# Decoder attention with rotary embedding: halves of each head from a second projection, or swapped by DMA from the third block on

## The chip, the cores and the metric

The kernel runs on one core of a Trainium2 chip. A core has five engines with queues of their own, each in order: PE (TensorE, matmuls into PSUM), DVE (VectorE), ACT (ScalarE), POOL (GpSimd) and SP (SyncE, which here only issues DMAs). They meet through semaphores. DMAs issued by SP, ACT or POOL move data beside them. The metric is the device time of one execution in microseconds (us), lower is better; the time of a kernel is the median of several runs. All times below are from the start of the profiled span.

## The reference, cut to what matters

A network of four layers, each a graph attention over 2708 nodes with a dense adjacency, followed by a feed-forward part that differs from layer to layer. The change touches only the feed-forward part of the third layer, a decoder block: causal attention over the 2708 nodes as one sequence (T = 2708, C = 256, 4 query heads and 2 key heads of 64), with a rotary embedding of q and k, and then a mixture of eight experts, two for each node.

```python
def _rotate_half(x):
    h = x.shape[-1] // 2
    return jnp.concatenate([-x[..., h:], x[..., :h]], axis=-1)
...
h = _rmsnorm(x, ln1_w)
q = (h @ wq.T).reshape(Bx, Tx, NH, HD).transpose(0, 2, 1, 3)
k = (h @ wk.T).reshape(Bx, Tx, NKV, HD).transpose(0, 2, 1, 3)
v = (h @ wv.T).reshape(Bx, Tx, NKV, HD).transpose(0, 2, 1, 3)
q = q * cos + _rotate_half(q) * sin
k = k * cos + _rotate_half(k) * sin
...
scores = jnp.einsum('bhtd,bhsd->bhts', q, k) / jnp.sqrt(jnp.float32(HD))
scores = jnp.where(causal[None, None], scores, jnp.float32(-1e+30))
att = jax.nn.softmax(scores, axis=-1)
y = jnp.einsum('bhts,bhsd->bhtd', att, v).transpose(0, 2, 1, 3).reshape(Bx, Tx, Cx)
x = x + y @ wo.T
```

## The kernel before

All numbers are float32. The whole network is one program; the function `attention` (line 1981) does the decoder's attention and calls the experts at its end.

**Tiling.** The 2708 nodes are cut into six column blocks, n = 0 to 5: five of 512 nodes and a last one of 148 (`cols`). Queries of a block are handled against all key tiles of 128 nodes up to the diagonal. A step (n, p, j) is one block n, one pair p of query heads and one key tile j. A pair holds one query head for each of the two key heads, each on 64 of the 128 partitions. In blocks 0 to 4 the two pairs are separate; in block 5 both go in one step (m = 2).

**A step.** `scores` multiplies the key tile with the queries on PE (line 2108, `sc`), takes the exp on ACT (line 2117, `e`) and masks diagonal tiles on VectorE (line 2123). `values` multiplies V with `e` on PE (line 2133, `po`) and adds `e` to a running sum on VectorE (line 2139, `sum`). `e` has four buffers, which are free again when that sum has read them. After a pair's last key tile, `close` sums over partitions on PE (`pd`, line 2147) and divides on VectorE (lines 2152 and 2153, `yt`).

**The projection of a block.** `project(n)` (line 2035) is a generator, run in small pieces between the steps of the block before. It norms the block's rows, transposes them (`tp`, line 2052, copied to `ft` by ACT, line 2056), projects V (`pv`, copied by ACT at line 2063), and then for k and the two pairs of q does this: for m = 0 and m = 1 it multiplies `ft` with columns of the weight into PSUM (line 2079, `pj`), the columns for m = 1 being those of m = 0 with the halves of each head exchanged; VectorE multiplies the two products with the cosine and with the signed sine (line 2082, `kt` or `qt`, and `tmp`); GpSimd adds the two (line 2083). The tables come by a DMA on ACT's queue (`rope`, line 2039).

**Closing work.** `send(n)` (line 2155) takes a closed block through the output projection (`wy`, line 143 in the trace as the matmuls are made by a helper; line 2170 on VectorE adds the residual, `xa`; line 2171 on GpSimd adds into X), the second norm (`h`, line 2183, and the chain of small operations `rr` in `inverse_root`), the router (`pr`, `dlogits`, line 2208) and `route.chunk`, which finds each node's slots (`rank`, `dto`) and scatters its rows to `hs` in DRAM by indirect DMAs on GpSimd's queue (line 1759). `route.keep` stores X to DRAM on SP's queue (line 1792, `dys<-X`). After block 2 (`CUT`), `route.cut` fixes the first eight expert tiles, and `route.load` reads them from `hs` on SP's queue (line 1907, `X<-hs`, eight loads of 130 KB).

**What sets the order.** On PE the order is the program's, written out by hand: `scores` of two steps, a piece of `send`, `values` of the two steps before, `close`, and then as many pieces of `project` as the count at line 2278 allows (its factor of 18 spreads the pieces over the steps of a block). On the other engines and on SP a scheduler orders the instructions ahead of time. `pj`, `pv`, `tp`, `pr`, `wy` and `pd` share one PSUM pool of two buffers (`aux`), used in turn. `tmp` has two buffers.

**After the attention.** When block 5 has been projected, `last_project` closes the pools of the projection, and `weights.more` loads the experts' w1 (line 1621) into the room that they leave; w3 follows at the attention's end. The experts (`h`, line 2349) start then.

Of the kernel before, what the change touches and what calls it, by code (L numbers as in the profile page):

```python
# [8 lines left out]
F32 = mybir.dt.float32  # L9
# [3 lines left out]
ALU = mybir.AluOpType  # L13
# [3 lines left out]
P = 128  # L17
# [31 lines left out]
def tiles_of(start, length):  # L49
    return range(start // P, (start + length + P - 1) // P)  # L50
# [1930 lines left out]
def attention(net, route, ln2, router, weights, mixture):  # L1981
# [7 lines left out]
    nc, tc, a, X = net.nc, net.tc, net.a, net.X  # L1989
    G, DH, CUT = 2, 64, 2  # L1990
    cols = chunks(512)
    halves = (slice(0, DH), slice(DH, P))
    with ExitStack() as ctx:
# [5 lines left out]
        aux = core.enter_context(tc.tile_pool(name="a_x", bufs=2, space=PSUM))  # L1999
# [5 lines left out]
        for t0, t1 in ((0, 4), (4, 12), (12, NT)):  # L2005
            g = slice(t0, t1)
# [28 lines left out]
        def project(n):  # L2035
            i0, iw = cols[n]
            its = tiles_of(i0, iw)
            rope = pp.tile([P, 2, 512], F32, name="rope")
            nc.scalar.dma_start(rope[:, :, :iw], a["rope"][:, :, i0 : i0 + iw].rearrange("n p i -> p n i"))
            ft = pp.tile([P, 2, 512], F32, name="ft")  # L2040
            fs = {}
            for t in its:
                fs[t] = pp.tile([P, D], F32, name="f", bufs=4)
                net.normed(fs[t], t, (ln[0], both))
            yield
            for k in range(0, len(its), 2):
                pair = its[k : k + 2]
                ps = aux.tile([P, 2, 2 * P], F32, name="tp", tag="aux")
                for m, t in enumerate(pair):
                    r, f = rows(t), fs[t]  # L2050
                    for c in range(2):
                        nc.tensor.transpose(
                            ps[:, c, m * P : m * P + r], f[:r, c * P : (c + 1) * P], net.ident[:r, :r]
                        )
                nw = (len(pair) - 1) * P + rows(pair[-1])
                nc.scalar.copy(ft[:, :, k * P : k * P + nw], ps[:, :, :nw])
                yield
            ps = aux.tile([P, 4, G, DH], F32, name="pv", tag="aux")
            for k, t in enumerate(its):
                r = rows(t)  # L2060
                net.matmul_k(ps[:r, k].rearrange("p g d -> p (g d)"), ft[:, :, k * P : k * P + r], wv)
            for k0, k1, r in whole_and_rest(its):
                nc.scalar.copy(V[:r, its[k0] : its[k1 - 1] + 1], ps[:r, k0:k1])

            if n + 1 < len(cols):
                queries[n] = [qp.tile([P, 1, 512], F32, name=f"qt{p}") for p in range(2)]
                pairs = [q[:, 0, :] for q in queries[n]]
            else:
                queries[n] = [qp.tile([P, 2, iw], F32, name="qt0")]
                pairs = [queries[n][0][:, p, :] for p in range(2)]  # L2070
            for dst, w in [(kt[:, i0 : i0 + iw], wk)] + [
                (pairs[p], wq[:, :, p * 2 * P : (p + 1) * 2 * P]) for p in range(2)
            ]:
                yield
                tmp = pp.tile([P, 512], F32, name="tmp")
                for m, part in enumerate((dst, tmp[:, :iw])):
                    ps = aux.tile([P, 512], F32, name="pj", tag="aux")
                    for c in range(2):
                        nc.tensor.matmul(  # L2079
                            ps[:, :iw], w[:, c, m * P : (m + 1) * P], ft[:, c, :iw], start=c == 0, stop=c == 1  # L2080
                        )
                    nc.vector.tensor_tensor(part, ps[:, :iw], rope[:, m, :iw], ALU.mult)
                nc.gpsimd.tensor_tensor(dst, dst, tmp[:, :iw], ALU.add)

        def by_pairs(t, m, iw):

# [160 lines left out]
        with tc.manual_schedule(engines={mybir.EngineType.PE}):  # L2247
# [10 lines left out]
            for group in groups + [[]]:  # L2258
                while group and group[-1][0] not in ready:
                    next(heads)  # L2260
                if group and group[0][0] > at[0]:
                    at[:] = group[0][0], 0, 0
                for step in group:
                    exp = scores(*step)
                next(tails, None)
                for step in before:
                    values(*step)
                if at[0] + 1 == len(cols):
                    next(tails, None)
                quiet -= 1  # L2270
                for n, p in ending:
                    close(n, p)
                    quiet = 2
                    if p + 1 == len(queries[n]):
                        closed.append(n)
                ending = [(n, p) for n, p, j in before if j == tiles_of(*cols[n])[-1]]
                at[1] += 1
                while group and at[2] * len(queries[at[0]]) * (tiles_of(*cols[at[0]])[-1] + 1) < at[1] * 18:
                    if quiet > 0 and at[0]:
                        break  # L2280
                    at[2] += 1
                    next(heads, None)
                before = group
# [434 lines left out]
```

## Time and profile before

| | |
|---|---|
| median of three runs | 2539.14 us (2534.76 to 2540.16) |
| the profiled execution | 2543.42 us |
| its span on the core | 2541.7 us |
| PE busy | 2403.5 us, 95% |
| VectorE busy | 1495.4 us, 59% |
| ACT busy | 1058.9 us, 42% |
| GpSimd busy | 438.9 us, 17% |
| decoder attention, first projection to experts | about 1496 to 1861 us |
| projections `pj` (line 2079) | 144 matmul records, 1496.0 to 1793.1 us |
| their multiplies on VectorE (line 2082) | 36, 0.69 us each for 128x512 |
| their adds on GpSimd (line 2083) | 18, 1.27 us each for 128x512 |
| `sc` and `po` of a group of two full steps on PE | 1.99 and 1.94 us |

Each float32 matmul shows as two records on PE. A line of the timeline has the start, the length from the first start to the last end, the engine, the line, the operation with its tiles and shapes and the number of records; idle time of the engine ahead of it stands in brackets with what ended it. As matmuls overlap, what a group costs is best taken from its start to the next group's start. A row of a stretch has its length and, for each engine, busy time and count. The waits list who waited for whom: total, times, longest.

### The profile page before, as it was taken

To read this page: it belongs to the slowest core of one execution; us is meant where nothing else is said; L and a number is where in the kernel's file an instruction comes from. 1 tells how busy PE (TensorE), PEld (TensorE's weight loads), DVE (VectorE), ACT (ScalarE), POOL (GpSimd) and SP (SyncE) were. 2 spreads that over 40 slices of the span, in tenths; PEclk is the share of its full clock that TensorE was granted. 3 is DMA by queue.
4 is the path that set the end of the run, shared out by engine and by line. 5 is a ranking of instruction groups with operands and counts; after the bars stand their busy time and mean duration, and the time that the engine had idled before them with its cause. 6 is when DMAs were issued, how large, how long until landed. Compare 5 with 4: busy or idle time off the path is not lost.

```text
span 2541.7 us, 32517 instructions
## 1 busy us (share of the span) xinstructions
PE 2403.5 (95%) x11437; PEld 1565.4 (62%) x11437; DVE 1495.4 (59%) x3446; ACT 1058.9 (42%) x1762; POOL 438.9 (17%) x581
## 2 busy tenths in 40 slices
PE   6899998989999999989899999999989999979999
PEld 5567665677233334568678864434467777757887
DVE  7753346837799996335544457788862222243666
ACT  3444443323788882332444333334422222234444
POOL 1000003201221222244230001222232122210011
PEclk9999999969899999989999999999999999989999
DMA  8899612000374764676520010001342222150001
GB/s 281 294 296 342 208 47 74 1 6 1 65 106 84 96 100 146 168 180 218 199 79 1 1 32 25 28 26 43 114 126 42 34 34 34 26 169 7 1 1 44
DMA packets 130276, 240.10 MB, mean 94 GB/s; under 512 B 10941, under 2 KB 76052, under 8 KB 127274
## 3 DMA queue, kind: packets, MB, share of 16 engines
q1 hardware_dynamic: 97440, 162.11, 20.0%
q0 software_dynamic: 29680, 71.77, 14.2%
q10 hardware_dynamic: 2990, 4.06, 0.6%
q8 instruction: 97, 1.59, 0.3%
q14 instruction: 69, 0.57, 0.1%
HBM read 146.52 MB, written 91.37 MB: 94 GB/s over the span
## 4 chain that ended last, share of the span: by engine, by line
PE 81%; DVE 10%; DMA 4%; ACT 2%; issue 1%; POOL 1%; SPq 0%; DVEq 0%; ACTq 0%; POOLq 0%
PE acc L1535 15%; PE acc L941 8%; PE h L2349 8%; PE acc L311 7%; PE po L2381 4%; PE score L298 4%; PE den L951 3%; PE y L1279 3%; PE sc L2108 3%; PE pv L143 3%; PE po L2133 3%; PE h L1138 3%; PE pj L2079 2%; DVE sum L2139 2%; DMA dys<-y,to 2%; PE po L143 2%
## 5 line engine op out<-in xcount | busy, mean ns | idle before, releaser
L1535 PE MATMUL acc<-V,e 128*128 128x257 f32 x1848 | 404.3, 381 | 5.8 <-DVE e L737 5.8
L1535 PEld LDWEIGHTS acc<-V,e 128*128 128x128 f32 x1848 | 351.3, 190 | 58.5 <-issue 6.6
L737 DVE SCALAR_TENSOR_TENSOR e<-e,low,mask 128x1172 f32<-128x1172 f32 (+1 forms) x176 | 273.7, 1622 | 21.4 <-ACT e L736 21.3
L736 ACT ACTIVATE e<-big_p,minus,ratio 128x1172 f32<-128x1172 f32 (+1 forms) x176 | 250.5, 1504 | 44.9 <-PE den L951 44.2
L737 DVE SCALAR_TENSOR_TENSOR e<-e,mask 128x768 f32<-128x768 f32 (+1 forms) x176 | 153.6, 875 | 171.2 <-ACT e L736 170.1
L736 ACT ACTIVATE e<-big_p,minus_one,ratio 128x768 f32<-128x768 f32 (+1 forms) x176 | 166.2, 947 | 210.5 <-PE acc L1535 189.9
L2349 PE MATMUL h<-w,ft 128*128 (+1 forms) x720 | 222.1, 450 | 0.0
L311 PE MATMUL acc<-F,e 128*128 128x257 f32 (+1 forms) x924 | 212.5, 383 | 4.2 <-DVE e L307 3.8
L941 PE MATMUL acc<-e,V 128*64 128x512 f32 (+1 forms) x1056 | 209.6, 549 | 1.3 <-DVE e L737 1.3
L311 PEld LDWEIGHTS acc<-F,e 128*128 128x128 f32 (+1 forms) x924 | 171.6, 189 | 57.0 <-DVE e L307 29.7
L2366 DVE TENSOR_TENSOR hh<-hh,h 128x682 f32<-128x682 f32 x47 | 40.7, 867 | 240.4 <-PE h L2349 240.4
L941 PEld LDWEIGHTS acc<-e,V 128*64 128x64 f32 x1056 | 73.7, 138 | 150.5 <-issue 146.0
L307 DVE TENSOR_TENSOR e<-e,mask 128x512 f32<-128x512 f32 (+2 forms) x132 | 80.4, 621 | 139.4 <-ACT e L300 137.7
L2349 PEld LDWEIGHTS h<-w,ft 128*128 128x128 f32 x720 | 129.1, 189 | 52.2
L2117 ACT ACTIVATE e<-sc 128x1024 f32<-128x1024 f32 (+4 forms) x131 | 107.4, 862 | 116.7 <-PE sc L2108 91.7
L2139 DVE TENSOR_TENSOR sum<-sum,e 128x1024 f32<-128x1024 f32 (+4 forms) x131 | 138.2, 1055 | 19.6 <-PE po L2133 11.4
L300 ACT ACTIVATE e<-score 128x512 f32<-128x512 f32 (+2 forms) x132 | 69.4, 544 | 171.0 <-PE score L298 145.5
L2381 PE MATMUL po<-w,ht 114*128 (+1 forms) x564 | 129.7, 379 | 0.9 <-DVE ht L2374 0.9
L2108 PE MATMUL sc<-qt,kt 64*128 64x512 f32 (+5 forms) x568 | 121.6, 546 | 1.4 <-ACT sum L2117 0.9
L2381 PEld LDWEIGHTS po<-w,ht 114*128 114x128 f32 x564 | 106.5, 189 | 22.6 <-DVE ht L2374 8.3
L298 PE MATMUL score<-QK 128*128 128x512 f32 (+2 forms) x264 | 112.1, 553 | 3.4 <-ACT e L300 3.0
L2133 PE MATMUL po<-e,V 128*64 128x512 f32 (+5 forms) x524 | 107.5, 527 | 1.7 <-DVE e L2123 1.7
(686 smaller groups left out, 3664.3 us busy)
## 6 DMA issues: line engine op xcount, KB each, us to landing
row<-in_adj SPq DMA_DIRECT2D x21, 1354.0 KB
raw<-in_adjT SPq DMA_DIRECT2D x35, 768.0 KB
sums<-e POOLq DMA_DIRECT2D x76, 330.0 KB
hs<-zero SPq DMA_DIRECT2D x8, 2860.0 KB
mask<-kept SPq DMA_DIRECT2D x42, 338.5 KB
hidden<-hr SPq DMA_DIRECT2D x32, 256.0 KB
wd<-in_f_wd SPq DMA_DIRECT2D x8, 1024.0 KB
kept<-mask SPq DMA_DIRECT2D x21, 338.5 KB
```

Of the source, the lines that this page charges most:

```text
L143: self.nc.tensor.matmul(out, lhsT[:, c, :], rhs[:, c, :], start=first and c == 0, stop=last and c == n - 1)
L298: nc.tensor.matmul(ps[:r, :iw], QK[:, 0, span(j)], QK[:, 1, i0 : i0 + iw], start=True, stop=True)
L311: ended = nc.tensor.matmul(acc[k], e[:r, k * P : (k + 1) * P], F[:r, j, :], start=j == 0, stop=j == NT - 1)
L736: nc.scalar.activation(v, big_p[:, i], AF.Relu, bias=minus, scale=ratio)
L737: return nc.vector.scalar_tensor_tensor(v, v, plus, net.mask[:, j, i], ALU.add, ALU.mult)
L941: nc.tensor.matmul(acc[n][half, :iw], V[:, j, h, :], e[n][:, k, :iw], start=j == 0, stop=j == NT - 1)
L1535: nc.tensor.matmul(acc[k][:ri], e[:, k * P : k * P + ri], V[:, j, :], start=j == 0, stop=j == NT - 1)
L2108: nc.tensor.matmul(by_pairs(ps[:r, g], m, iw)[:, :, o:], kt[b, span(j)], qt[b, :, o:iw], start=True, stop=True)
L2133: nc.tensor.matmul(by_pairs(outs[n, p][b], m, iw)[:, :, o:], V[:r, j, g, :], by_pairs(e[:r, g], m, iw)[:, :, o:], start=j == 0, stop=j == ...
L2139: nc.vector.tensor_tensor(total, total, by_heads(e[:r], m, iw)[:, :, :, o:], ALU.add)
L2349: last = nc.tensor.matmul(halves[s, n][:, q, :HALF], fts[s][:, c, :], weights.w13[n][:, es[s], c, q * HALF : (q + 1) * HALF], start=c == 0 ...
L2381: last = nc.tensor.matmul(ps, ht[:KP, k, :], w2[:KP, es[s], k, :], start=k == 0, stop=k == KC - 1)
```

## The change

From block 2 on, the second product (m = 1) is not computed. ACT copies the first product from PSUM to a new tile `plain` (two buffers), four DMAs on SP's queue copy 32 partitions each from `plain` to `tmp` with neighbouring groups of 32 exchanged, and VectorE multiplies `tmp` with the sine table in place. This multiply and GpSimd's add are put off: they are called in the next piece of the projection (`waiting`), those of the last pair in one more piece at the end. The count of pieces has the factor 20 instead of 18. Blocks 0 and 1 keep both products. The weights keep the exchanged columns.

```diff
--- before.py
+++ after.py
@@ -2068,19 +2068,40 @@
             else:
                 queries[n] = [qp.tile([P, 2, iw], F32, name="qt0")]
                 pairs = [queries[n][0][:, p, :] for p in range(2)]
+            waiting = []
             for dst, w in [(kt[:, i0 : i0 + iw], wk)] + [
                 (pairs[p], wq[:, :, p * 2 * P : (p + 1) * 2 * P]) for p in range(2)
             ]:
                 yield
                 tmp = pp.tile([P, 512], F32, name="tmp")
-                for m, part in enumerate((dst, tmp[:, :iw])):
-                    ps = aux.tile([P, 512], F32, name="pj", tag="aux")
+
+                def product(m):
+                    ps = aux.tile([P, 512], F32, name="pj", tag="aux")[:, :iw]
                     for c in range(2):
-                        nc.tensor.matmul(
-                            ps[:, :iw], w[:, c, m * P : (m + 1) * P], ft[:, c, :iw], start=c == 0, stop=c == 1
-                        )
-                    nc.vector.tensor_tensor(part, ps[:, :iw], rope[:, m, :iw], ALU.mult)
-                nc.gpsimd.tensor_tensor(dst, dst, tmp[:, :iw], ALU.add)
+                        nc.tensor.matmul(ps, w[:, c, m * P : (m + 1) * P], ft[:, c, :iw], start=c == 0, stop=c == 1)
+                    return ps
+
+                def turned(dst=dst, tmp=tmp[:, :iw], src=None):
+                    nc.vector.tensor_tensor(tmp, tmp if src is None else src, rope[:, 1, :iw], ALU.mult)
+                    nc.gpsimd.tensor_tensor(dst, dst, tmp, ALU.add)
+
+                ps = product(0)
+                if n > 1:
+                    plain = pp.tile([P, 512], F32, name="plain")
+                    nc.scalar.copy(plain[:, :iw], ps)
+                    for g in range(0, P, 32):
+                        nc.sync.dma_start(tmp[g : g + 32, :iw], plain[g ^ 32 : (g ^ 32) + 32, :iw])
+                nc.vector.tensor_tensor(dst, ps, rope[:, 0, :iw], ALU.mult)
+                if n > 1:
+                    for late in waiting:
+                        late()
+                    waiting[:] = [turned]
+                else:
+                    turned(src=product(1))
+            if n > 1:
+                yield
+            for late in waiting:
+                late()
 
         def by_pairs(t, m, iw):
 
@@ -2275,7 +2296,7 @@
                         closed.append(n)
                 ending = [(n, p) for n, p, j in before if j == tiles_of(*cols[n])[-1]]
                 at[1] += 1
-                while group and at[2] * len(queries[at[0]]) * (tiles_of(*cols[at[0]])[-1] + 1) < at[1] * 18:
+                while group and at[2] * len(queries[at[0]]) * (tiles_of(*cols[at[0]])[-1] + 1) < at[1] * 20:
                     if quiet > 0 and at[0]:
                         break
                     at[2] += 1
```

The compiled order of the changed program, set beside the one before: on PE nothing but the `pj` groups, `pv` of blocks 3 and 4 and the last block's second q projection has another place, `pj` being halved from block 2 on (the two q projections of block 2 now stand together). On SP the twelve swaps of block 2 stand ahead of the first `dys<-X`, twelve ahead of the second, eight ahead of the third, then four, the eight `X<-hs`, the four swaps of k of block 5, the fourth `dys<-X`, the last eight swaps and the loads of w1.

## The prediction

> **What bounds the kernel now.** I read the shares and the chain of waits first: PE is busy 95% of the span and 81% of the chain that ended last, so time is lost or won where PE's queue gets shorter or waits. Then I cut the decoder attention into stretches (columns: length, then busy time and count of PE, PEld, DVE, ACT and POOL, clock, DMA share, GB/s):
>
> ```profile
> 1545.00:1595.00 50.00, 49.22 (x228) 22.69 (x226) 38.60 (x77) 19.44 (x30) 6.92 (x7) 1.00 0.07 22
> 1595.00:1660.00 65.00, 63.42 (x294) 27.75 (x292) 51.97 (x117) 25.41 (x39) 16.98 (x15) 1.00 0.08 28
> 1660.00:1745.00 85.00, 82.03 (x372) 33.47 (x370) 67.48 (x162) 33.93 (x49) 17.35 (x15) 1.00 0.06 19
> 1745.00:1815.00 70.00, 69.33 (x338) 29.32 (x334) 59.58 (x136) 31.73 (x45) 18.65 (x18) 1.00 0.35 123
> ```
>
> In these 270 us, where all that the change touches runs, PE is busy for 264.0, DVE for 217.6 (81%), ACT for 110.5 (41%). PE bounds, at clock 1.00; DVE is close behind, ACT is not. Blocks are counted as in the code, n = 0 to 5; the change acts on n = 2 to 5.
>
> **What is removed.** PE's timeline gives a projection as eight matmul records, four of which are the second product:
>
> ```profile
> 1604.80 3.70 PE L2079 MATMUL pj<-ft,wk 128*128 128x512 f32 x8
> 1608.43 1.99 PE L2108 MATMUL sc<-qt,kt 64*128 64x512 f32 x8
> ...
> 1757.09 1.27 PE L2079 MATMUL pj<-ft,wk 128*128 128x148 f32 x8
> 1758.30 1.99 PE L2108 MATMUL sc<-qt,kt 64*128 64x512 f32 x8
> ```
>
> From start to next start a full block's costs 3.63 us, so half is 1.81; the last block's costs 1.21, half is 0.60. Blocks 2, 3 and 4 drop nine halves (16.3 us), block 5 three (1.8 us): **18.1 us** of PE, all in its own queue. Two waits for a PSUM buffer of the same pool also shrink: 1.57 us ahead of the q projection at 1631.12 (the order of instructions now puts VectorE's add `xa` earlier there; I take 0.9 as gone) and 0.58 at 1792.64, whose projection moves forward. Together -19.6 us.
>
> **What is added beside other work.** Twelve ACT copies out of PSUM: nine at 0.585 us (the row `V<-pv` 128x512), three shorter, under 6 us together. ACT idles for 101 us of the 270 behind PE's scores, which hides them: nothing. If that cover went, each would hold the next exp by at most 0.6 us, 6 us in all. VectorE keeps its count: the second multiply reads SBUF instead of PSUM, 0.691 us for the PSUM form against 0.684 for a row of the same size that reads SBUF alone (`sum<-sum,e` 128x512): nothing. GpSimd's twelve adds stay, later. The extra step per block and the factor 20 for 18 move projections by a step or two in PE's order and add no instruction.
>
> **The swaps.** 48 DMAs on SP's queue, four to a tile. One issue costs 0.43 us (median of `X<-hs`). No row shows an SBUF-to-SBUF transfer of 64 KB; the nearest is a 128 KB load on the same queue, from issue to the first instruction that uses it:
>
> ```profile
> 2258.32 4.70 SPq L1974 DMA_DIRECT2D X<-dys  x9
> ...
> 2260.44 0.43 DVE L164 BATCH_NORM_STATS2 bnst<-X 128x6 f32<-128x256 f32 x1 [5.93 <-DMA X<-dys]
> ```
>
> That is 2.1 us. The other bound is the 512 KB `dys<-X` on this queue, at the 300 to 400 GB/s that the w1 load reaches about 1.5 us of moving more, 3.6 us; I take 2.1, whose size is nearest. So a tile is swapped 0.6 + 3 x 0.43 + 2.1 = 4.0 us after its product. The late multiply waits for it on VectorE, whose queue is in order: everything behind stands too, above all the running sums (which free the exp buffers) and `xa` (which frees PSUM for PE). I placed each late multiply in the order that the changed program has on VectorE, and compared. For k of block 2 both come at about 1555; q pair 0 of block 2 waits some 1.9 us where VectorE now idles 2.22 us for `wy`; q pair 1 has 10 us to spare; for k of blocks 3 and 4 the swap is late by 0.4 to 1.2 us; for q pair 0 of blocks 3 and 4 it arrives within 0.3 us of the end of the sum ahead of it; q pair 1 of both has 1 us or more, also in block 4, where its swaps stand on SP behind the store `dys<-X` (1710.16); both q pairs of block 5, pair 0 again behind a `dys<-X`, are late by about 0.5 to 1. I put 2 us on all eleven (0 if they arrive 0.5 us sooner, 9 if 1 us later). Behind the swaps on SP come only those stores and the loads of w1, which go when the last add is done (1795 today) and are needed at 1861: 45 us of cover beyond the 20 or so that they take. The multiply of q pair 0 now also lies between the last sums and the reciprocals of a closing pair, a place where PE waits in block 4 (1.90 us for `yt`): +0.7 us.
>
> **The twelfth, k of block 5,** is another matter. In SP's new order its four swaps stand behind the eight loads `X<-hs`, which wait for scattered rows:
>
> ```profile
> SPq L1907 <- DMA hs<-h,dto: 55.0, 1, 55.0
> ```
>
> ```profile
> 1751.87 1.92 POOL L1759 DMA_INDIRECT hs<-h,dto  x1 [35.54 <-DVE h L1757]
> ...
> 1763.07 1.02 POOL L1759 DMA_INDIRECT hs<-h,dto  x1 [0.30 <-issue]
> ```
>
> ```profile
> 1765.57 3.67 SPq L1907 DMA_DIRECT2D X<-hs  x8
> ```
>
> The scatters start when VectorE has the slots, take GpSimd 12 us, and only then do the loads go, 8.5 us after this projection's start; nothing in the change moves that distance. So the first swap is issued at 1769.24, the last at 1770.5, landed at about 1772.7. VectorE comes to the late multiply at 1761:
>
> ```profile
> 1758.01 0.30 DVE L2082 TENSOR_TENSOR kt<-pj,rope 128x148 f32<-128x148 f32 x1
> 1758.40 0.31 DVE L2082 TENSOR_TENSOR tmp<-pj,rope 128x148 f32<-128x148 f32 x1
> 1760.53 1.24 DVE L2139 TENSOR_TENSOR sum<-sum,e 128x1024 f32<-128x1024 f32 x1 [1.81 <-issue]
> 1761.69 0.41 DVE L2170 TENSOR_TENSOR xa<-wy,xa 128x256 f32<-128x256 f32 x1
> ```
>
> It stands for nearly 12 us. Behind it are `xa` of the first two output tiles; PE needs their PSUM for the third at 1765.71 (1765.1 without the half). It gets it at 1772.7 + 0.3 (multiply) + 0.4 (`xa`) = 1773.4. Then `xa`, sum, `xa`, two `h`, mask, sum, mask, `xa` of the third tile run as now, 6.5 us of VectorE from 1773, before the q projection that now starts at 1769.50 (1768.9) finds a buffer: 1779.3. **PE loses 10.4 us there**; later both engines stand to each other as before, so it is not won back (between 1780 and 1797 VectorE's closing chain and PE share the path). Bounds: 7 us if loads and swaps land 3 us sooner, 14 if 3 us later.
>
> After a gap PE also runs slow. Today's 4.28 us gap is followed by:
>
> ```profile
> 1858.00:1860.00 2.00, 0.21 (x2) 0.21 (x4) 0.30 (x2) 0.37 (x1) 1.12 (x2) 0.50 0.18 67
> 1860.00:1862.00 2.00, 2.00 (x6) 0.88 (x5) 0.91 (x1) 0.37 (x1) 0.00 (x0) 0.50 0.18 67
> ```
>
> A gap of 8 us should do the same for some 4.6 us, as there (1859.8 to 1864.4). Most of it falls where PE waits for VectorE anyway: at half speed the two output tiles and the values behind them end near 1780 instead of 1778, and the buffer comes at 1779.3. I take +0.8 us. The Trainium skill, "TensorE: Matmul & The Clock Gate", Part 1, has the clock halve after one idle window of about 3.4 us and come back after as long a busy one. By that rule the 8 us gap surely halves it, but only for 3.4 us, and the 0.8 would be near nothing, the sum -6.5. The trace is less tidy: 0.50 is also granted at 1848 to 1850, soon after a gap of only 1.57 us.
>
> **Sum.** -18.1 - 0.9 - 0.6 + 0.7 + 2.0 + 10.4 + 0.8 = **-5.7 us**. The profiled execution took 2543.42 us (span 2541.7), 4.3 above the median of the three runs, 2539.14. It gives 2537.7 there, and 2533.5 on the median.
>
> **Rivals.** (a) *The stall is hidden.* PE alone decides and the twelfth swap costs little: -18.1 - 1.5 + 0.7 + 2 = -17, 2522. For it: PE's 98%. Against: SP's queue cannot pass the loads, and the `xa` that PE needs lie behind the wait. (b) *The landing of the swaps decides: slower.* Place: the seven waits that arrive within a microsecond (k of 2, 3, 4, q pair 0 of 3 and 4, both q of 5), in a VectorE that would be 86% busy (217.6 of 252). Price: some 6 us for each microsecond of landing beyond 2.1; from 3.0 us on the change costs time, at 4.1 it is +6, 2545. For it: no row for such a transfer, four issues to a tile. Against: light DMA load (6 to 8%) up to 1745. (c) *VectorE becomes the bound:* after each closing pair it already holds the path (1617 to 1631, 1649 to 1667, 1691 to 1708); if half of the remaining gain turns into waits for it, -2, 2537. That the change doesn't do what it says can be left out: PE's order in the changed program lacks the matmuls.
>
> **How the numbers follow.** Forecast 45% (-10 to -1), (a) 17%, (b) 25%, (c) 13%. What a measurement of this kernel can tell from no change is about 0.2%, 5.1 us, and the forecast lies just beyond: I give 25 of its 45 to faster, 20 to the same. (a) is faster, (c) the same, (b) slower but for 5. Faster 0.42, same 0.38, slower 0.20. The range, 2522 to 2546, takes in (a) and most of (b).
>
> **What would show it.** Right: `pj` has half its records in blocks 2 to 5; VectorE waits some 12 us for a DMA ahead of one 128x148 multiply, shortly after `X<-hs`; PE has one gap of about 8 us before `wy` there, with clock 0.50 after it. Wrong: no such gap (a), or waits of 1 to 3 us for DMA ahead of most late multiplies (b). Most in doubt are the landing time and the part of the stall that PE sees.

## The result, and the profile after

| | before | after |
|---|---|---|
| median of the runs | 2537.51 us (2528.78 to 2540.93, 14 runs) | 2541.61 us (2536.48 to 2547.41, 14 runs) |
| ratio of the times, 95% interval | 1 | 1.0021 (1.0012 to 1.0031), or +5.3 us (+3.0 to +7.9) |
| the profiled execution, its span | 2543.42, 2541.7 us | 2538.90, 2536.9 us |
| PE busy, matmul records | 2403.5 us, 11437 | 2382.3 us, 11389 |

The change costs some 5 us where 5.7 less were forecast. PE does what was foreseen: it is busy 21 us less. But it does not finish sooner. All differences below in microseconds are a ratio times 2537.5.

The attention in four parts again, cut near the places where PE had reached the same work before (at 1733 that fits; the cuts at 1590, 1655 and 1815 lie some 4, 5 and 2 us behind it; columns: length, then busy time and count of PE, PEld, DVE, ACT and POOL, clock, DMA share, GB/s):

```profile
1540.00:1590.00 50.00, 47.63 (x240) 22.99 (x236) 44.43 (x83) 22.40 (x35) 8.33 (x7) 1.00 0.14 38
1590.00:1655.00 65.00, 60.59 (x276) 25.17 (x276) 56.47 (x125) 27.35 (x41) 19.74 (x15) 0.97 0.13 40
1655.00:1733.00 78.00, 75.45 (x340) 30.52 (x336) 61.79 (x148) 34.95 (x50) 16.56 (x15) 0.96 0.10 31
1733.00:1815.00 82.00, 71.89 (x340) 29.92 (x338) 59.50 (x138) 33.32 (x50) 22.52 (x20) 0.94 0.31 109
```

PE now idles 19.4 us of 275 where it idled 6 of 270, and its clock, 1.00 in all four parts before, is 0.97, 0.96 and 0.94 in the last three. From the attention's first transposition to block 5's first scores (`sc` of 64x296), two marks that both kernels have, this execution takes 327.6 us where the one before took 324.5. Two things are to be looked for: gaps, and slow matmuls behind them. A projection itself is halved as foreseen; PE's timeline has four records each for k of block 4 and of block 5:

```profile
1665.81 1.98 PE L2081 MATMUL pj<-ft,wk 128*128 128x512 f32 x4
...
1744.90 0.77 PE L2081 MATMUL pj<-ft,wk 128*128 128x148 f32 x4
```

PE's waits between 1540 and 1815 (total, times, longest) give the gaps:

```profile
PE wy L143 <- DVE xa L2191: 9.1, 1, 9.1
PE pj L2081 <- DVE xa L2191: 3.1, 1, 3.1
PE wy L143 <- DVE yt L2173: 2.5, 1, 2.5
```

and VectorE's in the same stretch what VectorE itself stood for:

```profile
DVE tmp L2085 <- DMA tmp<-plain: 19.3, 9, 12.5
DVE qt L2094 <- ACT plain L2091: 4.6, 4, 3.1
```

Of 19.3 us that VectorE waits for swaps, 12.5 are one wait, that of block 5's k. The other eight share 6.8. The second line was not foreseen: VectorE's first multiply waits for ACT's copy, though both only read the product. The program names the copy first; where it names the multiply first, in a run below, ACT waits for VectorE instead.

**The stall of block 5** is the forecast one. On SP the swaps stand behind the loads of scattered rows:

```profile
1753.96 3.68 SPq L1907 DMA_DIRECT2D X<-hs  x8
1757.76 2.41 SPq L2093 DMA_DIRECT2D tmp<-plain  x4
```

VectorE reaches the late multiply at 1749.06 and stands until the swaps have landed:

```profile
1761.52 0.31 DVE L2085 TENSOR_TENSOR tmp<-tmp,rope 128x148 f32<-128x148 f32 x1 [12.46 <-DMA tmp<-plain]
1761.75 0.42 DVE L2191 TENSOR_TENSOR xa<-wy,xa 128x256 f32<-128x256 f32 x1
```

and PE, whose third output tile needs the buffer that this `xa` frees, has a gap and then half speed (eight records of `wy` take 1.99 us at full clock, of `po` 1.94):

```profile
1762.22 3.78 PE L143 MATMUL wy<-wo,yt 128*128 128x256 f32 x8 [9.14 <-DVE xa L2191]
1765.93 2.42 PE L2154 MATMUL po<-e,V 128*64 128x512 f32 x8
```

9.14 us of gap and 1.79 + 0.48 of slow matmuls are 11.4 us; 10.4 + 0.8 had been forecast.

**What was not foreseen** stands in blocks 3 and 4, where the first queries' late multiply lies ahead of the closing division. VectorE around the closing of block 3:

```profile
1680.41 0.69 DVE L2085 TENSOR_TENSOR tmp<-tmp,rope 128x512 f32<-128x512 f32 x1 [0.72 <-DMA tmp<-plain]
1681.02 1.22 DVE L2160 TENSOR_TENSOR sum<-sum,e 128x1024 f32<-128x1024 f32 x1
1682.15 3.36 DVE L2173 RECIPROCAL yt<-pd 128x256 f32<-128x256 f32 x2
1685.43 0.68 DVE L2174 TENSOR_TENSOR yt<-yt,po 128x256 f32<-128x256 f32 x2
```

PE waits for that `yt`, and so at the closing of block 2 for the `xa` behind it. Before the change the two places looked like this:

```profile
1631.12 3.70 PE L2079 MATMUL pj<-ft,wq 128*128 128x512 f32 x8 [1.57 <-DVE xa L2170]
...
1698.86 1.10 PE L143 MATMUL wy<-wo,yt 128*128 128x256 f32 x4 [1.90 <-DVE yt L2152]
1699.89 1.94 PE L2133 MATMUL po<-e,V 128*64 128x512 f32 x8
```

and now:

```profile
1620.64 3.43 PE L2081 MATMUL pj<-ft,wq 128*128 128x512 f32 x4 [3.13 <-DVE xa L2191]
...
1685.66 2.05 PE L143 MATMUL wy<-wo,yt 128*128 128x256 f32 x4 [2.55 <-DVE yt L2173]
1687.64 3.68 PE L2154 MATMUL po<-e,V 128*64 128x512 f32 x8
1691.25 2.27 PE L2129 MATMUL sc<-qt,kt 64*128 64x512 f32 x8
```

VectorE's waits for the swap are under a microsecond at these two closings, but the two gaps of PE, 1.57 and 1.90 us before, are now 3.13 and 2.55. And the matmuls behind them are slow: 3.43 us for 1.98, 2.05 for 1.10, 3.68 for 1.94, 2.27 for 1.99. The clock (the number ahead of the last two columns) says why:

```profile
1684.00:1686.00 2.00, 0.34 (x1) 0.37 (x2) 2.00 (x3) 0.00 (x0) 0.58 (x1) 0.76 0.00 0
1686.00:1688.00 2.00, 2.00 (x6) 1.11 (x7) 1.36 (x6) 0.51 (x2) 0.73 (x1) 0.50 0.03 8
1688.00:1690.00 2.00, 2.00 (x6) 0.47 (x4) 2.00 (x4) 0.51 (x2) 1.63 (x1) 0.50 0.00 0
1690.00:1692.00 2.00, 2.00 (x6) 0.51 (x4) 2.00 (x5) 0.00 (x0) 0.00 (x0) 0.54 0.00 0
1692.00:1694.00 2.00, 2.00 (x11) 0.88 (x8) 1.47 (x3) 1.23 (x2) 0.00 (x0) 1.00 0.00 0
```

This gap of 2.55 us is followed by some 6 us at half clock, which cost 3.0 us, more than the gap itself.

### The profile page after: what moved, and what is told of

The parts are those of the page before. It is cut to its first block, busy times and chain, and to the rows that moved or that the text cites. A ratio compares the mean times of both kernels' runs of the same rounds, so it can differ in the third digit from the quotient of the medians.

```text
span 2536.9 us, 32558 instructions
## 1 busy us (share of the span) xinstructions
PE 2382.3 (94%) x11389; PEld 1553.4 (61%) x11389; DVE 1499.8 (59%) x3446; ACT 1066.0 (42%) x1774; POOL 444.7 (18%) x581
## 3 DMA queue, kind: packets, MB, share of 16 engines
q8 instruction: 97, 1.59, 0.3%
## 4 chain that ended last, share of the span: by engine, by line
PE 78%; DVE 11%; DMA 5%; ACT 2%; issue 2%; POOL 1%; SPq 0%; DVEq 0%; ACTq 0%; POOLq 0%
PE acc L1535 15%; PE acc L941 8%; PE h L2370 8%; PE acc L311 7%; PE po L2402 4%; PE score L298 4%; PE den L951 3%; PE y L1279 3%; PE pv L143 3%; PE h L1138 3%; PE po L2154 2%; PE sc L2129 2%; DVE sum L2160 2%; DMA dys<-y,to 2%; PE pj L2081 2%
```

## The experiments

| kernel | ratio to before (95%) | us |
|---|---|---|
| changed kernel | 1.0021 (1.0012 to 1.0031) | +5.3 |
| before again | 0.9997 (0.9984 to 1.0010) | -0.8 |
| only half the products, nothing added | 0.9939 (0.9919 to 0.9960) | -15.5 |
| changed, without the DMAs | 0.9946 (0.9930 to 0.9961) | -13.7 |
| changed, products in block 5 | 0.9981 (0.9969 to 0.9993) | -4.8 |
| the same, multiplies behind the closing | 0.9954 (0.9938 to 0.9971) | -11.7 |
| the same once more | 0.9936 (0.9910 to 0.9961) | -16.2 |
| the same, block 1 swapped too | 0.9955 (0.9941 to 0.9969) | -11.4 |
| swaps in all four blocks, multiplies moved | 0.9943 (0.9915 to 0.9970) | -14.5 |
| changed, multiply ahead of the copy | 1.0013 (1.0002 to 1.0025) | +3.3 |
| changed, block 5 on ACT's queue | 1.0007 (0.9994 to 1.0020) | +1.8 |
| changed, swaps on two queues | 1.0023 (1.0011 to 1.0034) | +5.8 |
| changed, eight swaps to a tile | 1.0003 (0.9990 to 1.0016) | +0.8 |

My theory after the result was: the stall of block 5 costs 11 us, the swaps of blocks 2 to 4 some 9 to 10, because VectorE comes late and PE then runs at half clock. The main rival was that the landing time itself is what is paid, as in case (b) of the prediction.

### Products in block 5

```diff
-                if n > 1:
+                if 1 < n < 5:
```

(in all three places)

> The changed kernel, but block 5 keeps its two products; blocks 2 to 4 are swapped. Theory (the wait of the twelfth swap, behind the scattered rows on SP, costs PE 11 us and the other eleven some 9 to 10): about 9 us less than the changed kernel (11 won, 1.8 of halves given back), so 3 to 5 us under the kernel before, ratio 0.998 to 0.999. Rival (that stall is won back later, and the loss lies in the swaps of blocks 2 to 4): no more than 2 us off the changed kernel, ratio 1.001 to 1.003. In the profile PE's gap of 9 us ahead of wy near 1761 should be gone under either.

Measured -4.8 us, 10.1 less than the changed kernel; PE's gap of 9 us is gone. With the 1.8 us of halves that were given back the stall cost 11.9. The theory holds; the rival, that it is won back later, falls.

### Without the DMAs

```diff
-                    for g in range(0, P, 32):
-                        nc.sync.dma_start(tmp[g : g + 32, :iw], plain[g ^ 32 : (g ^ 32) + 32, :iw])
...
-                    waiting[:] = [turned]
+                    waiting[:] = [lambda turned=turned, src=plain[:, :iw]: turned(src=src)]
```

> The changed kernel without its 48 DMAs: the late multiply reads plain itself, so the halves are not exchanged. All else (copies on ACT, order, late adds) stays. Theory: without the 11 us stall and without most of the 7 us that VectorE waits for the other swaps, 13 to 16 us less than the changed kernel: 8 to 11 under the kernel before, ratio 0.9957 to 0.9969; what then lacks to -19 is VectorE's wait for ACT's copy and PE's half clock. Rival 1 (waits for swaps are all of the loss): 17 to 20 under the kernel before, ratio 0.992 to 0.993. Rival 2 (the loss is VectorE's and ACT's own, the swaps cost little): no more than 5 under it, ratio 0.998 or above.

Measured -13.7 us (-17.8 to -9.9), between the theory's -8 to -11 and the first rival's -17 to -20; the second rival falls. So copies, order and late adds cost little (1.8 us against the next kernel, which is within the error), and the swaps cost 19 us in all: 11.9 in block 5, the remaining 7 in blocks 2 to 4.

### Half the products, nothing added

```diff
                 for m, part in enumerate((dst, tmp[:, :iw])):
-                    ps = aux.tile([P, 512], F32, name="pj", tag="aux")
-                    for c in range(2):
...
+                    if not m or n < 2:
+                        ps = aux.tile([P, 512], F32, name="pj", tag="aux")
+                        for c in range(2):
...
```

> The kernel before with one thing changed: from block 2 on the second product is left out and the second multiply reads the first product once more, so the halves are not exchanged; nothing is put off, copied or swapped. It prices the halves of PE alone. Theory: the 18.1 us are on PE's path: 16 to 19 under the kernel before, ratio 0.9925 to 0.9937. Rival (VectorE, 81 to 86% busy, becomes the bound and takes back half): 6 to 11 under it, ratio 0.9957 to 0.9976.

Measured -15.5 us (-20.6 to -10.2). On PE's timeline this kernel gains 17.6 us from the first projection to the last `pd` of block 4. The halves are on PE's path, as the prediction had it, and VectorE is no new bound.

### The multiply ahead of the copy

```diff
                 ps = product(0)
+                nc.vector.tensor_tensor(dst, ps, rope[:, 0, :iw], ALU.mult)
                 if n > 1:
...
-                nc.vector.tensor_tensor(dst, ps, rope[:, 0, :iw], ALU.mult)
```

> The changed kernel with VectorE's first multiply written ahead of ACT's copy, so that VectorE waits for PE alone and ACT's copy, and with it the swap, goes about 0.7 us later. If the 4.6 us that VectorE waits for the copy are what PE loses in blocks 2 to 4: 3 to 5 us less than the changed kernel, ratio 1.000 to 1.001. If the landing of the swaps is what counts: 2 to 5 us more, ratio 1.003 to 1.004. My own guess is that the two nearly cancel: within 2 us of the changed kernel.

Measured +3.3 us, 2 less than the changed kernel with intervals that overlap. The edit did more than it was meant to: with the swaps later, the scheduler put the first queries' multiplies of blocks 3 and 4 behind the closing divisions by itself (that of block 3 still ahead of `xa`). What that won was lost in other places. ACT now waits for VectorE with its exps behind it:

```profile
1637.82 0.59 ACT L2092 COPY plain<-pj 128x512 f32<-128x512 f32 x1 [3.91 <-DVE qt L2089]
```

PE has new gaps there, of 2.29 us ahead of `wy` at 1638 and 1.76 ahead of `sc` at 1645, and one of 2.38 ahead of `po` at 1578 with slow scores behind it (3.41 us for 1.99). So this run does not price the wait for the copy by itself.

### Two queues

```diff
-                        nc.sync.dma_start(tmp[g : g + 32, :iw], plain[g ^ 32 : (g ^ 32) + 32, :iw])
+                        (nc.scalar if n < 5 and g > 32 else nc.sync).dma_start(tmp[g : g + 32, :iw], ...)
```

> The changed kernel with two of the four swaps of each tile of blocks 2 to 4 issued from ACT's queue, block 5 as it was: the last swap is issued about 1.2 us earlier. Theory (what blocks 2 to 4 lose is the time from the copy's end to the landing, 3.9 to 4.7 us where 3.4 was forecast, at some 6 us for each microsecond): 4 to 7 us less than the changed kernel, ratio 0.9995 to 1.0007. Rival (the issues cost ACT what VectorE wins, as exps stand behind an issue that waits for GpSimd's last add on the buffer): within 2 us of the changed kernel or above, ratio 1.0013 or more.

Measured +5.8 us, as the changed kernel. The theory's 1.2 us never came: in block 4 the multiply of the first queries still begins 4.0 us after the copy's end (4.3 in the changed kernel), and ACT pays for its two issues. ACT's timeline at that place:

```profile
1676.96 0.59 ACT L2091 COPY plain<-pj 128x512 f32<-128x512 f32 x1 [1.62 <-issue]
1677.63 1.36 ACTq L2093 DMA_DIRECT2D tmp<-plain  x2
1679.10 1.94 ACT L2138 ACTIVATE e<-sc 128x1024 f32<-128x1024 f32 x2 [1.55 <-issue]
```

The exp begins when the issues are done, and PE's gap ahead of `wy` at that closing is 6.03 us, where it was 2.55. As the landing was hardly changed, the run says nothing on its price; the next one does.

### Eight swaps to a tile

```diff
-                    for g in range(0, P, 32):
-                        nc.sync.dma_start(tmp[g : g + 32, :iw], plain[g ^ 32 : (g ^ 32) + 32, :iw])
+                    for g in range(0, P, 32 if n == 5 else 16):
+                        z = 32 if n == 5 else 16
+                        nc.sync.dma_start(tmp[g : g + z, :iw], plain[g ^ 32 : (g ^ 32) + z, :iw])
```

> The changed kernel with eight swaps of 16 partitions in place of four of 32 for each tile of blocks 2 to 4, block 5 as it was: at 0.6 us an issue on SP the last part lands about 2.4 us later, with the same bytes. Theory (time from copy to landing is what blocks 2 to 4 pay for, at some 6 us for each microsecond): 8 to 15 us above the changed kernel, ratio 1.005 to 1.008. Rival (the waits are paid once, by half clock after gaps that are there anyway, and further delay is mostly hidden): no more than 4 us above it, ratio 1.0036 or less.

Measured +0.8 us: not 8 to 15 above the changed kernel but 4.6 below it. This was the run that I had most wrong. The swaps do land later: k of blocks 3 and 4 begins its late multiply 7.4 and 7.1 us after the copy's end, where it was 4.7 and 3.9. But with this edit the scheduler, which orders VectorE ahead of time, puts the first queries' multiplies behind the closing divisions. VectorE and PE at the closing of block 3:

```profile
1696.39 0.68 DVE L2085 TENSOR_TENSOR tmp<-tmp,rope 128x512 f32<-128x512 f32 x1
```

```profile
1690.94 1.10 PE L143 MATMUL wy<-wo,yt 128*128 128x256 f32 x4 [1.33 <-DVE yt L2174]
1691.98 1.94 PE L2155 MATMUL po<-e,V 128*64 128x512 f32 x8
```

The multiply comes after `yt` and waits for nothing, PE's gap is 1.33 us, and the matmuls behind it run at full clock. (At the closing of block 2 it now stands ahead of `xa`, and PE's gap of 3.38 us and the slow `pj` stay.) So the price of 6 us for each microsecond of landing falls, and with it my own expectation. What costs is the place of the waiting multiply in VectorE's order.

### Multiplies behind the closing

This had been tried by itself on the kernel with products in block 5:

```diff
                     for late in waiting:
-                        late()
+                        with tc.issue_after(ended[0].ins):
+                            late()
```

(both loops; it moves only the multiplies of the first queries of blocks 3 and 4)

> The kernel with two products in block 5 and swaps in blocks 2 to 4, and the late multiplies ordered on VectorE behind the last finished closing: this moves only those of q pair 0 of blocks 3 and 4, from ahead of the reciprocals to behind xa. Theory (the swap waits of 0.93 and 0.72 us and the multiplies' 0.69 us ahead of the reciprocals lengthen two gaps of PE from 2.46 to 3.13 and from 1.33 to 2.55 us, after which PE runs at half clock for 3 to 5 us): both half clocks go, 2 + 5 us won less what the multiply costs in its new place, so 3 to 6 us under the kernel with two products in block 5, ratio 0.9957 to 0.9969. Rival (the waits come to the same wherever the multiply stands): no more than 1.5 us off that kernel, ratio 0.9975 to 0.9985.

Measured -11.7 us, 6.9 less than its base, and -16.2 (-22.8 to -9.9) in a second comparison. VectorE and PE at the closing of block 3, to be held against the lines of the changed kernel above:

```profile
1677.18 3.36 DVE L2175 RECIPROCAL yt<-pd 128x256 f32<-128x256 f32 x2
...
1686.14 0.68 DVE L2085 TENSOR_TENSOR tmp<-tmp,rope 128x512 f32<-128x512 f32 x1
```

```profile
1680.69 1.10 PE L143 MATMUL wy<-wo,yt 128*128 128x256 f32 x4 [1.33 <-DVE yt L2175]
1681.72 1.94 PE L2156 MATMUL po<-e,V 128*64 128x512 f32 x8
```

The multiply stands 9 us behind the start of the division and PE does not wait for it; PE's two gaps are 1.59 and 1.33 us and no matmul is slow. Against the changed kernel that is 1.54 + 1.22 us of gaps and 1.45 + 0.95 + 1.74 + 0.28 of half clock, 7.2 us. In the three other profiles of the changed kernel the same sum is 5.3, 7.3 and 8.0 us and in the base's own 5.5, so the 6.9 of the runs lies among them.

### Block 5 on ACT's queue

```diff
-                        nc.sync.dma_start(tmp[g : g + 32, :iw], ...)
+                        (nc.scalar if n == 5 else nc.sync).dma_start(tmp[g : g + 32, :iw], ...)
```

> The changed kernel with the twelve swaps of block 5 issued from ACT's queue instead of SP's, so that those of k are not behind the eight loads X<-hs. Theory (the stall comes from the order on SP alone): VectorE's wait of 12.5 us is gone, 9 to 12 us less than the changed kernel, ratio 0.9975 to 0.9988. Rival (ACT, which holds its exps behind the issues, loses as much, or the stall sits elsewhere): no more than 4 us less, ratio 1.0005 or above.

Measured +1.8 us: 3.5 less than the changed kernel, not 9 to 12. VectorE's wait is gone, but another takes its place. ACT's timeline:

```profile
1747.32 0.28 ACT L2091 COPY plain<-pj 128x148 f32<-128x148 f32 x1 [1.48 <-PE pj L2081]
1757.19 2.53 ACTq L2093 DMA_DIRECT2D tmp<-plain  x4
1759.83 1.94 ACT L2138 ACTIVATE e<-sc 128x1024 f32<-128x1024 f32 x2 [12.23 <-DMA tmp<-plain]
```

and PE's:

```profile
1760.91 3.36 PE L2129 MATMUL sc<-qt,kt 64*128 64x512 f32 x8 [7.92 <-ACT e L2138]
```

No view of the trace names what the issue itself waited for; the compiled program does. In it the DMAs of SP and ACT take eight completion semaphores in turn, and an issue waits until the DMA that had its semaphore before has landed. The first swap of k follows the first `X<-hs` (issued at 1754.98) on its semaphore, so ACT stood until 1757.19 for the same scattered rows, and its exps behind it. In this program another queue was not another order, as the two queues share their semaphores.

### Swaps in all blocks, the multiplies moved

```diff
-                tmp = pp.tile([P, 512], F32, name="tmp")
+                tmp = pp.tile([P, 512], F32, name="tmp", bufs=3)
...
-                    for late in waiting:
-                        late()
-                    waiting[:] = [turned]
+                    for late in waiting[: 0 if n == 5 else None]:
+                        with tc.issue_after(ended[0].ins):
+                            late()
+                    waiting[:] = [turned] + waiting if n == 5 else [turned]
...
             for late in waiting:
-                late()
+                with tc.issue_after(ended[0].ins):
+                    late()
```

> The change in all its blocks, block 5 too, on the same order of SP: only VectorE's late multiplies are moved, those of q pair 0 of blocks 3 and 4 behind the closing, and all three of block 5 into the last piece, k's last (one more buffer for tmp). Theory (a swap that lands late costs nothing if the multiply that waits for it stands where nothing behind it is needed; the loss is the place): no stall of 9 us at the third output tile, and the 1.8 us of block 5's halves on top of the kernel with products in block 5: 12 to 15 us under the kernel before, ratio 0.994 to 0.9955. Rival (the order on SP is the cause: the swaps hold something else up when they land late, the scores of block 5 for one): 3 us or more above the kernel with products in block 5, ratio 0.997 or above.

> The kernel with products in block 5 and late multiplies behind the closing, timed on the same chip as its variant with all swaps: ratio 0.9945 to 0.9965 as before, 1 to 3 us above the variant if the place of the multiply is all that matters.

Measured -14.5 us, and -16.2 for its base beside it: no difference that these intervals can tell (1.8 us were hoped for). What matters is that the stall is gone with SP's order as it was:

```profile
1756.21 3.69 SPq L1907 DMA_DIRECT2D X<-hs  x8
1760.01 2.41 SPq L2093 DMA_DIRECT2D tmp<-plain  x4
```

```profile
1755.02 1.99 PE L143 MATMUL wy<-wo,yt 128*128 128x256 f32 x8
1756.95 1.94 PE L2156 MATMUL po<-e,V 128*64 128x512 f32 x8
1758.82 0.77 PE L2081 MATMUL pj<-ft,wq 128*128 128x148 f32 x4
```

The swaps of k still leave SP at 1760, behind the loads, but their multiply now stands last, at 1780.57, and the third output tile follows without a gap. (The trace has a new gap further on, of 1.81 us ahead of scores at 1787.53, with `po` in 3.27 us for 1.94 behind it; the base's three traces don't have it, and part of the 1.8 us may have gone there.) So the order on SP made the swap late, and the place on VectorE made the lateness cost 11 us. The whole change, with its four swapped blocks, is some 14 us faster than the kernel before (-21.6 to -7.6) once the multiplies stand where nothing behind them is needed.

### Block 1 swapped too

`0 < n < 5` in place of `1 < n < 5`, on the kernel with multiplies behind the closing.

> The best kernel so far (swaps in blocks 2 to 4, products in block 5, late multiplies behind the last finished closing) with block 1 swapped too. Block 1 is projected beside the few steps of block 0, and its keys are needed some 10 us after their product. Theory (a swap costs nothing where its 4.2 us and the late operations fit ahead of the use): three more halves of 1.81 us won, 3 to 5 us under that kernel, ratio 0.9935 to 0.9945. Rival (they don't fit: VectorE or PE waits for them): the same or up to 6 us above it, ratio 0.9955 to 0.9978.

Measured -11.4 us (-15.0 to -7.9), the same as its base in the first comparison: the middle is the rival's, though the interval reaches into the theory's range. PE's timeline has a place where gain goes, a gap of 2.30 us ahead of block 1's first scores, for the late add of the second queries:

```profile
1528.27 1.99 PE L2131 MATMUL sc<-qt,kt 64*128 64x512 f32 x8 [2.30 <-POOL qt L2086]
```

### Where the rest lies

Taken as a whole, the changed kernel's attention is no slower in the profiles than that of before. I repeated both kernels for their profiles.

> The kernel before once more, to see how far one profiled execution stands from the next. Its profiled execution of before took 2543.42 us, near the top of its runs, and has a gap of 4.28 us on PE ahead of pd at 1859.79 which no other kernel's profile has. Theory (that gap is a chance of that one execution, not a property of the kernel): a profiled time of 2534 to 2540 without the gap. Rival (the change removed the gap, and something else costs what the profiles don't show): the gap of 4 us is there again. Ratio to before 1.000 within 0.0012 either way.

> The changed kernel once more, for a second profile. From attention's first transposition to the experts' start its profiled execution took 386.0 us and the two of before 386.6 and 386.8, though the medians are 4 to 5 us apart. Theory (that stretch repeats to some tenths, and the difference lies in what comes before it, which varies by 10 us and more from one execution to the next): 386 within 0.5 us here. Rival (the first profile was a lucky one, and PE falls to half clock after more of its gaps in other executions): 388 to 392 us here.

> The changed kernel a third time, for a third profile, with the same expectations: 386 within 0.5 us for the stretch if it repeats; 388 to 392 if the first profile was a lucky one.

> The kernel before, for another profile. Theory (the stretch ahead of the attention is longer in the changed kernels): attention begins 3 to 6 us earlier here than in the two changed kernels beside it, and PE's wait for hr near 1115 is about 5 us, not 12. Rival (that wait belongs to the chip or the moment): the same wait and the same start in all four, within 3 us.

> As the run before it: attention begins 3 to 6 us earlier than in the two changed kernels if the kernels differ there, within 3 us of them if the chip or the moment decides. The attention itself takes 384.1 to 384.3 us again.

> The changed kernel, for another profile beside two of before on one chip: attention begins 3 to 6 us later than in those if the kernels differ ahead of it, within 3 us if not; the attention itself takes 380 to 384 us again, by how many of PE's gaps are followed by half clock.

> The best kernel so far (products in block 5, late multiplies behind the last finished closing) for a second profile: attention begins as late as in the changed kernel if kernels differ ahead of it, and takes 368 to 370 us again, with no stretch of half clock between 1600 and 1700.

| profiles | attention begins at | from there to the first `tp` of X in the experts |
|---|---|---|
| before, four | 1490.8, 1482.6, 1490.5, 1489.3 | 384.1, 384.3, 380.5, 384.1 |
| after, four | 1485.7, 1489.9, 1496.4, 1484.4 | 383.5, 380.3, 382.7, 387.9 |
| multiplies behind the closing, three | 1484.3, 1494.2, 1490.4 | 368.9, 373.1, 366.4 |

(The expectations count to a mark 2.5 us later, hence 386.) The stretch is 383.3 us on average before and 383.6 after, where the runs say +3.0 to +7.9. But the kernels do differ in the part that the change touches, up to block 5's first scores (`sc` of 64x296): 324.4 to 324.7 us in the four profiles of before, 327.6, 325.0, 327.4 and 328.1 in those of the changed kernel, and 310.7 to 311.6 with the multiplies behind the closing. That is +2.5 and -13.5 us on average, a little under the lower end of the runs' +3.0 to +7.9, and between the two comparisons of the runs (-11.7 and -16.2). The changed kernel does not repeat to tenths there: in the last of its profiles PE's gap for `yt` was 3.83 us instead of 2.55, in the second the first gap 2.68 instead of 3.13. The beginning of the attention varies by 14 us, in kernels of either kind, and the wait for `hr` near 1115 that I had suspected is 2.7 to 5.0 us on one chip in both kinds, 3.4 to 5.1 on two others and 10.9 to 13.6 on two more: it belongs to the chip or the moment. So neither theory of these runs is shown. Some 3 of the runs' 5 us are not in this part, and stay open.

What evens out the whole stretch lies in its tail. Three of four profiles of before, so not that first one alone, have a gap of some 4 us ahead of the last `pd`, behind a wait of ACT that the profile puts down to something outside the core's engines:

```profile
1859.37 0.37 ACT L2291 COPY X<-tp 128x256 f32<-128x256 f32 x1 [4.72 <-remote]
```

The profiles of the changed kernel don't have it there:

```profile
1853.69 0.72 PE L2168 MATMUL pd<-sum,ones 128*64 128x296 f32 x4 [0.24 <-ACT X L2312]
```

What ACT waits for there wasn't found out. It makes the stretch of before some 4 us longer (384.1 with it, 380.5 in the profile without). That the change takes it away is not shown: the kernel with block 5 on ACT's queue has such a wait of 4.75 us at ACT's next operation, the first of the experts.

## Why the prediction was wrong, point by point

- **The halves, -18.1, and two smaller waits, -1.5.** Right in size, within the error: -15.5 measured with nothing added, -20.6 to -10.2, and -17.6 in the trace. That leaves 2 to 4 of the 11 us between forecast and result here. The first of the two waits did not shrink: it is 1.58 us in the kernel with nothing added, and doubled in the changed one (1.57 to 3.13 us).
- **The twelfth swap, +10.4 and +0.8.** Right: 11.9 by the runs, 9.14 of gap and 2.27 of half clock in the trace. The half clock was sized too low. My reason, "SP's queue cannot pass the loads", was half of it: with the same order on SP the stall went when the multiply was moved.
- **The late multiply of the first queries at the closing, "a place where PE waits in block 4 (1.90 us for `yt`): +0.7 us".** This is the step that failed. The 0.7 is the length of the multiply alone, at one place. There are two, for the multiplies of blocks 3 and 4, and with the wait for the swap and the half clock they cost 6.9 us by the runs, 7.2 by the trace, against a kernel with those multiplies elsewhere: 2.8 of longer gaps, 4.4 of half clock behind them. I had counted the half clock behind the gap of 8 us alone. I had read in the trace of before that 0.50 is granted "soon after a gap of only 1.57 us", and yet asked of no other gap whether it would grow past such a bound.
- **The other swaps, +2.0.** With that place taken out, the kernel with swaps in blocks 2 to 4 is 2.0 us above the one without DMAs (-11.7 and -13.7), and 1.8 of it are the halves of block 5, which it computes. So the other swaps of these blocks cost about nothing: no more than forecast, as far as can be told.
- **The swap's time.** Forecast 3.4 us from the copy's end to the multiply, measured 3.9 to 4.7: an issue of these swaps takes 0.6 us on SP, not 0.43. By the prediction's own rule of 6 us for each microsecond that would be about what went wrong, and rival (b) would have won for its reason. The eight-swap kernel shows that it didn't: 7.1 us to the landing of k cost nothing that the runs can tell.
- **ACT's copies, nothing.** Right: the kernel without DMAs lies 1.8 us from the one without copies, within the error. (The 101 us that ACT idles behind PE's scores are those from 1540 to 1815; in the 270 us named they are 96.7. Nothing rests on the difference.)

Sum: -15.5 for the halves, 1.8 for copies and order, 0.2 for swaps in harmless places, 6.9 for the two multiplies at the closings and 11.9 for the last are +5.3. That it comes out exactly is arithmetic, as the terms are differences between these same kernels; each has an error of 3 to 4 us. Rival (a) is what the change would be with the multiplies elsewhere: 2522 forecast, 2523 by the ratio 0.9943. Rival (b) had the right sign for the wrong reason. (c), VectorE as the bound, is excluded by the kernel with half the products.

## What to carry to other kernels

A wait on an in-order engine is priced by what stands behind it, not by its length: a swap that left its queue 12 us late cost nothing where its multiply stood behind the work that others needed, and a wait of 0.7 us with a multiply of 0.7 cost PE 4 us in one execution at the head of the chain that it waits for. So when an operation is put off, look where the scheduler has put its second half, and order that half behind the work that another engine is waiting for. And ask of each gap of PE that grows whether it comes near 2.5 us, since behind such gaps the matmuls were slow here, and cost another 1.4 to 3.0 us.

## What the runs showed of the hardware

**The clock and the length of a gap.** PE's gaps at the closings of blocks 2 to 4 and ahead of the output tiles and projections, where it is busy on both sides, in all the kernels here (a length that comes again stands once):

| gap of PE, us | matmuls behind it |
|---|---|
| 1.33, 1.40, 1.57, 1.59, 1.67, 1.90, 2.11, 2.29, 2.46 | at full clock, every one |
| 2.48, 2.50, 2.55, 2.68, 2.90, 3.13, 3.27, 3.29, 3.38, 3.83, 3.87, 6.03, 7.92, 8.56, 9.14 | at half clock, every one |

In one of two gaps of 2.50 us the half clock begins 1 us after the gap's end (four records of `wy` in 1.10 us, then `po` in 3.45). Elsewhere shorter gaps were followed by slow matmuls. In the kernel with swaps in all blocks the gap of 1.81 us ahead of scores at 1787.53, with PE busy for 9 us ahead of it, was followed by `po` in 3.27 us for 1.94, at a clock of 0.50. Where several gaps lie close together, ahead of `po` near 1570, gaps of 1.94 and 2.38 us were followed by 2.31 and 1.95 us where 1.72 is usual. The Trainium skill, "TensorE: Matmul & The Clock Gate", Part 1 (What's actually happening), has the clock halve after an idle window of about 3.4 us that runs freely. Here 2.48 us were enough, and once 1.81, so as a rule for how long PE may stand, 3.4 us is too generous. At the places of the table the change lies between 2.46 and 2.48 us, with one gap so near on either side; that the length of a gap alone decides is not shown, and the 1.81 us speak against it. The slow stretch behind lasted some 3 to 6 us.

**Issuing a DMA** for 64 KB from SBUF to SBUF takes 0.6 to 0.7 us of its queue's engine in the median. On SP it holds up only other DMAs; on ACT the exps wait for it (1.36 us for two, 2.53 for four).

**Swaps of 16 partitions instead of 32** took 5.2 us of SP for eight, and landed 7.1 to 7.4 us after the copy, where four of 32 took 2.4 and 3.9 to 4.7: in these swaps the time goes by the number of DMAs, not by the bytes.
